# A four-layer graph network on one core: two more neighbour blocks gathered, operands moved in SBUF, rows asked for singly

## The chip, the core and the metric

The kernel runs on one NeuronCore of a Trainium2 chip. Its engines work side by side: TensorE (PE, with its weight loads PEld), VectorE (DVE), ScalarE (ACT), GpSimd (POOL) and SyncE (SP), which only starts transfers. The metric is the time of one execution on the device in microseconds, lower is better; the numbers of before are the median of three runs and one profiled execution.

## The reference

There are 6250 nodes of 256 features and 100000 edges, sorted by destination. Cut to what matters:

```python
def agg(h):
    return segment_sum(h[src], dst, num_segments=N)      # sum over a node's in-edges

h = maximum(layernorm(x), 0)
for l in range(3):
    t = relu((h + agg(h)) @ W1s[l] + b1s[l])
    t = relu(t @ W2s[l] + b2s[l])
    h = t @ W3s[l] + b3s[l]
t = relu((h + agg(h)) @ cW1 + cb1)
t = relu(t @ cW2 + cb2)                                   # 64 wide
return x + t @ cW3 + cb3
```

Since the sum over neighbours is linear, the kernel applies a layer's first weight matrix before it aggregates: W3 of one layer and W1 of the next are multiplied into one matrix, and each layer aggregates rows that are already weighted.

## The kernel before

The nodes lie in 49 blocks of 128. There are four aggregations, called layers 0 to 3 here. The features of all blocks are held in the tile `XY` (128 partitions x 49 blocks x 512 numbers): the first 256 numbers of a block are the features rounded for the fast matmul type (f32r), the other 256 are the remainder, so that two products together keep the precision.

A block of destinations is aggregated in one of two ways, which do not depend on each other:

- **Dense.** The number of edges from each source to each destination of a block is a count matrix, 49 x 128 x 128 bytes. In layer 0 it is built on the chip (`build`: one-hot rows on VectorE, L1034, multiplied at L1075, cast to bytes at L1083 and L1085) and stored to DRAM (`mats`); layers 1 to 3 fetch it again (`fetch`, L1105). Before a product the bytes are cast to f32r in a ring of tiles `a` (L1549 in layer 0, L1565 later). A panel of four blocks is one product of 49 x 4 matmuls with `XY` stationary and `a` moving (L1665); a single block ("solo", and every block in layer 0) is 49 matmuls with `a` stationary and `XY` moving (L1588). All of these are 128 x 128 by 512 columns.
- **Gathered.** For a block, 17 indirect DMAs (L1382) on the POOL queue each bring 128 rows of 1 KB, one per edge, from the DRAM copy of the features (`table`) into buffers `rows`. One-hot matrices (`one_hots`, L1402, on VectorE) and 23 small matmuls, 46 instructions in the trace (L1419), sum them in two "visits". L1439 and L1448 add the block itself.

Both ways end in the same rest: a transpose (L1479) or the product's own layout, ReLU, the second matmul (L1232), the third (L1289, in layer 3 L1244) and the store to the next table.

Which block goes which way stands in lists. `gone` (L468) are the groups that can be gathered, `panels` (L469) the dense panels, `teams` (L476) the dense blocks of layer 0 in order, `solos` (L470) the dense single blocks of layers 1 to 3, `stock` (L471) everything with a count matrix. `Gathered.blocks` (L1340) takes every block of `gone` that is not dense in that layer: 22 in layer 0, 18 in layers 1 and 2, 19 in layer 3, 77 in all and 77 x 17 = 1309 gathers. `order` (L1490) is the sequence of panels and solos in a layer.

The order of the work is written out by hand and instruction by instruction, with a planner's clock (`passed`) that adds fixed costs for what has been put on TensorE: `COLS` per column of a dense matmul, `VISIT`, `TURN` and others (L1508). From `work_of`, the planned length of a layer, `begin` derives `pace`, the planned time between two rows. `flow` (L1370) then asks for rows `LEAD` (21 us) before they are due; each gather carries a wait for the latest matmul (`after`, `paced`). In layers 1 to 3 the number asked for is rounded down to a multiple of `TRAIN`, 4. A visit is put between dense matmuls when its time on the clock has come (`meets`), or in any case in the last 8 units of a layer; if its rows have not been asked for, they are asked for there. A layer's first gather can only follow once the table of that layer is stored whole.

POOL does nothing but gathers in the layers. The row buffers are `gath` (24) in layer 0 and `gath2` (26) later. SyncE starts all other transfers.

Where the tiles lie in a partition follows from the order of the pools and the sizes in them. Before, `XY` starts at byte 16544, which is 160 modulo 256; the tiles `a` start at 193760 + k x 2048 (`rings`, layer 0; 224 modulo 256) and at 182688 + k x 2048 (`rings2`, layers 1 to 3; 160 modulo 256). The step from one block of `XY` to the next is 2048 bytes and from one stationary slice to the next 512 bytes, so these residues hold for every matmul of a kind.

Of the kernel before, what the change touches and what calls it, by code (L numbers as in the profile page):

```python
# [10 lines left out]
U8 = mybir.dt.uint8  # L11
# [6 lines left out]
P = 128  # L18
# [378 lines left out]
def sorted_edges(  # L397
# [69 lines left out]

    gone = [(0, 4), (4, 4), (8, 4), (12, 4), (16, 4), (44, 4), (48, 1)]  # L468
    panels = [(20, 4), (24, 4), (28, 4), (32, 4), (36, 4), (40, 4), (44, 4)]  # L469
    solos = [[], [17, 18, 19], [17, 18, 19], [18, 19]]  # L470
    stock = panels + [(b, 1) for b in solos[1]]  # L471
    place_of = {b + i: (p, i) for p, (b, n) in enumerate(stock) for i in range(n)}
    S0 = 2 * min(place_of)


    teams = [(17, 3), (20, 4), (24, 4), (28, 4), (32, 4), (36, 4), (40, 2), (42, 2)]  # L476
    made = [b + i for b, n in teams for i in range(n)]
    for i in range(panels[-1][1]):
        made.insert(6 * i + 5, panels[-1][0] + i)
# [7 lines left out]
    const = ctx.enter_context(tc.tile_pool(name="const", bufs=1))  # L487
    dram = ctx.enter_context(tc.tile_pool(name="dram", bufs=1, space=DRAM))
    ps_g = ctx.enter_context(tc.tile_pool(name="ps_g", bufs=1, space=PSUM))
    ps_m = ctx.enter_context(tc.tile_pool(name="ps_m", bufs=2, space=PSUM))  # L490

    XY = const.tile([P, NT, 2 * C], F32R, name="XY")
    ident = const.tile([P, P], F32, name="ident")
    clT = const.tile([P, 2, GSUB, NSUB - S0], BF16, name="clT")
# [111 lines left out]
    def ask(n):  # L606

        for _ in range(min(n, len(asks))):
            to, e, at = asks.pop(0)
            got = nc.gpsimd.indirect_dma_start(  # L610
                out=to, out_offset=None, in_=e.rearrange("(o e) -> o e", o=1),
                in_offset=bass.IndirectOffsetOnAxis(ap=at, axis=1),
            )
            after(got, "edges are asked for a few at a time")

    def look(pool):
# [200 lines left out]
        for w, (q0, q1) in ((3, (0, NQ - 1)), (4, (NQ - 1, NQ))):  # L817
            rows = gone[q0][1] * T
            nc.vector.tensor_reduce(wrong[:rows, w:w + 1], off[:rows, q0:q1, :],
                                    axis=mybir.AxisListType.XY, op=OP.max)  # L820
        ask(len(asks))
# [26 lines left out]
    def verdict():  # L848
        bad = ps_m.tile([P, W], F32, name="ps")
        nc.tensor.matmul(bad[:1, :5], one, wrong, start=True, stop=True)  # L850
        return bad

    def judge(bad):
        nc.vector.tensor_reduce(amiss, bad[:1, :5], axis=mybir.AxisListType.X, op=OP.add)
        nc.vector.tensor_scalar(good, amiss, 0.0, None, op0=OP.is_equal)


    def normed(pool, ps_t, ps_z):
# [54 lines left out]
        def times(s):  # L913
# [8 lines left out]
            if s == len(pairs) - 1:  # L922
                still = ps_m.tile([P, W], F32, name="ps")
                for _ in range(10):
                    nc.tensor.matmul(still, XY[:, 1, :P], XY[:, 0, :], start=True, stop=True)

# [6 lines left out]
        def high(s):  # L933
            i0, n = pairs[s]
            nc.scalar.copy(XY[:, i0:i0 + n, :C], zs[s][:, :n, :])

        def low(s):
            i0, n = pairs[s]
            nc.vector.tensor_tensor(XY[:, i0:i0 + n, C:], zs[s][:, :n, :],
                                    XY[:, i0:i0 + n, :C].bitcast(F32), OP.subtract)  # L940

# [21 lines left out]
    with tc.manual_schedule():  # L963
        with tc.tile_pool(name="prep", bufs=2) as prep, tc.tile_pool(
            name="ps_t", bufs=2, space=PSUM
# [146 lines left out]
        def later(n, fn):  # L1112
            due.append((now[0] + n, fn))
# [25 lines left out]
        def tick(layer):  # L1139

            now[0] += 1
            run = [f for t, f in due if t <= now[0]]
            due[:] = [(t, f) for t, f in due if t > now[0]]
            for f in run:
                f()
            visit = layer.meets()
            for task in list(jobs):
                first, last, fn = task
                if max(first, lock[0]) <= now[0] and (visit or last <= now[0]):
                    jobs.remove(task)  # L1150
                    fn()
            if queue:
                step(visit)
# [5 lines left out]
        def split(j, m, z):  # L1159

            nc.scalar.copy(XY[:, j:j + m, :C], z[:, :m, :])
            later(1, lambda: nc.vector.tensor_tensor(XY[:, j:j + m, C:], z[:, :m, :],
# [171 lines left out]
        class Gathered:  # L1334
# [35 lines left out]
            def flow(self):  # L1370

                if self.first is not None:
                    n = int((clock[0] - self.first + LEAD) / self.pace) + 1
                    self.send(n if n >= len(self.order) or not self.l else n - n % TRAIN)

            def send(self, upto):
                while self.sent < min(upto, len(self.order)):
# [109 lines left out]
        EARLY = 8  # L1487
        PRE = (GSUB + EARLY) // 2
        tails = [7] + [panels[-1][1]] * NLAYER
        order = [[]] + [[0, 17, 1, 18, 2, 3, 19, 4, 5, 6]] * 2 + [[0, 1, 18, 2, 3, 19, 4, 5, 6]]  # L1490
        order = [[p if p < len(panels) else place_of[p][0] for p in o] for o in order]
        nodes = [b + i for b, n in teams for i in range(n)]
        parts = [(j, 1) for j in range(NT)]
# [13 lines left out]
        LEAD, TAIL = 21.0, 10.0  # L1507
        COLS, FULL32, TURN, VISIT, BUILD, BURST = 0.457e-3, 1.68e-3, 0.4, 1.7, 0.2, 0.3  # L1508
        clock = [0.0]
        FAR, SPAN, TRAIN = 7, 6, 4  # L1510

        ends = [sum(1 for k, *_ in units if k <= l) for l in range(NLAYER + 1)]
        layers = [Gathered(l) for l in range(NLAYER + 1)]
# [98 lines left out]
        def product_of_team(b0, n, ps_a, beside, hurry):  # L1612
            us, h1 = [], []

            def turn(i, two):
                if not h1:
                    h1.append(work.tile([P, KC, W], F32, name="h1", bufs=2) if hurry else
                              ats.tile([P, KC, W], F32, name="h1", bufs=1))
                turned(0, two, h1[0], i)
                if i == n - 1:  # L1620
                    mlp(0, b0, n, h1[0], hurry, FAR)

            for i in range(n):
                us.append(spare[:, i * C:(i + 1) * C] if hurry else
                          ats.tile([P, C], F32, name="un", bufs=4))
                if not hurry:
                    product_by_node(0, (b0 + i,), ps_a, us[i:], beside)
                elif i == n - 1:
                    product_by_node(0, pieces[-1], ps_a, us, beside)
                if i % 2 or i == n - 1:  # L1630
                    two = us[i - i % 2:i + 1]
                    if hurry:
                        def soon(i=i, two=two):
                            if now[0] < lock[0] or sum(len(g["steps"]) == 2 for g in queue) > 1:
                                later(1, soon)
                            else:
                                turn(i, two)

                        later(3, soon)
                    else:  # L1640
                        job(FAR - 2, FAR - 2 + SPAN, lambda i=i, two=two: turn(i, two))
# [51 lines left out]
        with tc.tile_pool(name="hots", bufs=1) as hots, tc.tile_pool(  # L1693
            name="ats", bufs=1
        ) as ats, tc.tile_pool(name="rings", bufs=AHEAD + 2) as rings, tc.tile_pool(
            name="gath", bufs=24
        ) as gath, tc.tile_pool(
            name="ps_a", bufs=2, space=PSUM
        ) as ps_a, tc.tile_pool(name="ps_b", bufs=3, space=PSUM) as ps_b:
            begun = {0: clock[0]}  # L1700
            layers[0].begin()
            layers[0].send(layers[0].upto[1])
            beside = build(hots, ats, ps_b)
            while now[0] < PRE:
                for _ in range(2):
                    next(beside)
                    built[0] += 1
                tick(layers[0])
                layers[0].advance()
            later(1, lambda: later(2, lambda bad=verdict(): judge(bad)))  # L1710
            for team in teams:
                product_of_team(*team, ps_a, beside, team == teams[-1])
            assert next(beside, None) is None and built[0] == total
        chunks = ctx.enter_context(tc.tile_pool(name="chunks", bufs=1))
        late = ctx.enter_context(tc.tile_pool(name="late", bufs=1))
        rings = ctx.enter_context(tc.tile_pool(name="rings2", bufs=AHEAD + 6))
        gath = ctx.enter_context(tc.tile_pool(name="gath2", bufs=26))
        ps_a = ctx.enter_context(tc.tile_pool(name="ps_a2", bufs=4, space=PSUM))
        for l in range(1, NLAYER + 1):
            for p in order[l]:  # L1720
# [7 lines left out]
def kernel(  # L1728
# [26 lines left out]
    good = keep.tile([1, 1], I32, name="good")  # L1755
    rest = (x, src, dst, W1s, b1s, W2s, b2s, W3s, b3s, cW1, cb1, cW2, cb2, cW3, cb3, out)
    sorted_edges(tc, good, *rest)
    done = nc.values_load(good[0:1, 0:1], min_val=0, max_val=1)  # L1758
    with tc.If(done == 0):
# [27 lines left out]
```

## Time and profile before

| what | value |
|---|---|
| three runs | 2186.52 us median, 2184.53 to 2191.45 |
| profiled execution | 2191.15 us |
| its span, first to last instruction | 2189.4 us |
| mean granted TensorE clock | 0.986 |
| gathers (L1382) | 1309, mean 991 ns |
| dense matmuls (L1665 and L1588) | 4116 + 1715 |
| DMA, mean | 155 GB/s |

The span is some 2 us shorter than the execution, which holds the start and the end of the program as well. A matmul's duration in the trace (396 ns for a dense one) is longer than its distance to the next, because matmuls overlap in the array: what a matmul costs is read from how close two start. "Issue" is time in which an engine waited for nothing that the profile shows. SP and POOL rows with DMA names are the issuing, not the transfer.

### The profile page before, as it was taken

What the parts mean: (1) busy time and instruction counts of PE and PEld (TensorE: products, weight loads), DVE (VectorE), ACT (ScalarE), POOL (GpSimd) and SP (SyncE); (2) the same over time, 40 slices, a digit from 0 to 9 for tenths busy, and PEclk for the clock granted to TensorE, in tenths of its full rate; (3) what the DMA queues carried; (4) which work ended last, traced back from release to release, by engine and by line L of the source; (5) the groups of instructions that cost most, each with busy time, mean ns of one, the idle gap of its engine ahead of it and who ended that gap; (6) DMA issues with size and microseconds to landing.
All of it is one profiled execution on the core that took longest, in us unless ns stands there. A gap on an engine that the chain in (4) does not pass through costs nothing. (4 is left out here: it accounts for less than half of the span.)

```text
span 2189.4 us, 32889 instructions
## 1 busy us (share of the span) xinstructions
PE 2110.3 (96%) x12123; PEld 1530.8 (70%) x12123; DVE 951.4 (43%) x2230; ACT 892.6 (41%) x1834; POOL 1354.5 (62%) x1385
## 2 busy tenths in 40 slices
PE   4989999999999999999998999999999999999998
PEld 3756766667667777777775777777776677677675
DVE  7987767676663422222233322222223333233333
ACT  4856656565555523223333433232323333223222
POOL 2736666776763466666665266666666177777773
PEclk9989999999999999999999999999999999999999
DMA  4534444545445654445444544545455455566454
GB/s 156 169 103 147 143 143 143 155 138 153 146 147 163 189 158 146 148 136 173 149 153 141 173 152 136 166 137 167 129 164 174 134 173 190 180 195 187 155 176 130
DMA packets 182129, 340.44 MB, mean 155 GB/s; under 512 B 31246, under 2 KB 117296, under 8 KB 181958
## 3 DMA queue, kind: packets, MB, share of 16 engines
q0 software_dynamic: 64880, 174.27, 27.0%
q1 hardware_dynamic: 115150, 162.13, 22.5%
q8 instruction: 97, 1.59, 0.3%
q10 hardware_dynamic: 1928, 1.85, 0.3%
q14 instruction: 74, 0.61, 0.1%
HBM read 280.05 MB, written 58.07 MB: 154 GB/s over the span
## 5 line engine op out<-in xcount | busy, mean ns | idle before, releaser
L1382 POOL DMA_INDIRECT rows<-table,idx x1309 | 1297.7, 991 | 757.8 <-issue 272.7
L1665 PE MATMUL agg<-a,XY 128*128 128x512 f32 x4116 | 981.8, 396 | 2.0 <-ACT a L1565 2.0
L1665 PEld LDWEIGHTS agg<-a,XY 128*128 128x128 f32 x4116 | 767.5, 189 | 206.1 <-issue 37.3
L1565 ACT CAST a<-at 128x512 fp32r<-128x512 uint8 (+1 forms) x571 | 343.7, 616 | 594.7 <-PE agg L1665 537.8
L1565 DVE CAST a<-at 128x512 fp32r<-128x512 uint8 (+1 forms) x570 | 250.2, 442 | 563.6 <-PE agg L1665 462.6
L1588 PE MATMUL agg<-XY,a 128*128 128x512 f32 x1715 | 469.1, 410 | 0.6 <-ACT a L1549 0.6
L1588 PEld LDWEIGHTS agg<-XY,a 128*128 128x128 f32 x1715 | 305.0, 190 | 64.8 <-issue 10.9
L1419 PE MATMUL sums<-rows,hot 128*32 128x256 f32 x3542 | 249.1, 387 | 21.2 <-DMA rows<-table,idx 19.9
L1419 PEld LDWEIGHTS sums<-rows,hot 128*32 128x32 f32 x3542 | 107.0, 110 | 145.6 <-issue 53.2
L1549 ACT CAST a<-at 128x512 fp32r<-128x512 uint8 (+2 forms) x375 | 204.5, 575 | 6.2 <-PE agg L1588 6.2
L1083 ACT CAST at<-bp 128x392 uint8<-128x392 f32 x248 | 120.8, 488 | 202.1 <-PE bp L1075 193.8
L1085 DVE CAST at<-bp 128x392 uint8<-128x392 f32 x248 | 140.0, 565 | 139.4 <-PE bp L1075 138.4
L1448 DVE TENSOR_TENSOR u<-u,sums 128x256 f32<-128x256 f32 x77 | 32.3, 419 | 253.3 <-PE agg L1665 220.0
L1075 PE MATMUL bp<-hi,lo 128*128 128x196 bf16 x992 | 132.6, 255 | 9.9 <-DVE hi L1034 9.6
L1034 DVE TENSOR_TENSOR hi<-cols,pairs 128x784 bf16<-128x784 bf16 x248 | 139.3, 562 | 0.0
L1289 PE MATMUL ps<-w,h 128*128 128x256 f32 x588 | 133.9, 380 | 1.9 <-ACT h L1483 1.0
L1232 PE MATMUL ps<-h,w 128*128 128x512 f32 (+4 forms) x332 | 134.1, 546 | 0.7 <-DVE zz L1297 0.6
L1075 PEld LDWEIGHTS <-lo 128*128 128x128 bf16 x992 | 73.1, 99 | 84.8 <-DVE hi L1034 27.9
L1289 PEld LDWEIGHTS ps<-w,h 128*128 128x128 f32 x588 | 110.9, 190 | 18.5 <-ACT h L1483 1.5
L1483 ACT ACTIVATE h<-ps,bias 128x256 f32<-128x256 f32 (+1 forms) x118 | 47.5, 460 | 155.7 <-PE ps L1479 155.5
L1034 DVE TENSOR_TENSOR lo<-lanes,pairs 128x512 bf16<-128x512 bf16 x248 | 103.8, 419 | 1.3 <-ACT pairs L1029 1.3
L1232 PEld LDWEIGHTS ps<-h,w 128*128 128x128 f32 (+1 forms) x332 | 60.4, 189 | 54.7 <-issue 49.0
(171 smaller groups left out, 971.4 us busy)
## 6 DMA issues: line engine op xcount, KB each, us to landing
at<-mat SPq DMA_DIRECT2D x155, 448.0 KB
mat<-at SPq DMA_DIRECT2D x31, 784.0 KB
rows<-table,idx POOLq DMA_INDIRECT x1309
table<-zz SPq DMA_DIRECT2D x71, 256.0 KB
back<-table SPq DMA_DIRECT2D x99, 128.0 KB
xs<-in_x_dram SPq DMA_DIRECT2D x8, 768.0 KB
table<-zs SPq DMA_DIRECT2D x24, 256.0 KB
out_dram<-zz SPq DMA_DIRECT2D x24, 256.0 KB
```

Source lines behind the costliest of these rows:

```text
L1034: nc.vector.tensor_tensor(o.rearrange("p q (n t) -> p q n t", t=2), values.rearrange("p (n t) -> p n t", t=2)[:, None, :, :].to_broadcast( ...
L1075: mm = nc.tensor.matmul(bp[:, m * HW:(m + 1) * HW], lo[:, q + m, :], hi[:, q + m, :], start=True, stop=True)
L1083: nc.scalar.copy(o, v)
L1085: nc.vector.tensor_copy(o, v)
L1232: mm = nc.tensor.matmul(ps[:mp, :w], weights[l][0][:, c, i * P:i * P + mp], h1[:, c, :w], start=(c == 0), stop=(c == KC - 1))
L1289: mm = nc.tensor.matmul(o, h2[0][:, c, nodes], w3[:, c, :], start=(c == 0), stop=(c == KC - 1))
L1382: got = nc.gpsimd.indirect_dma_start(out=t, out_offset=None, in_=tables[self.l][:, :], in_offset=bass.IndirectOffsetOnAxis(ap=idx[:, o:o + ...
L1419: nc.tensor.matmul(self.sums[m * Q:(m + 1) * Q, :C], self.hot[:, (c - min(rounds)) // 2, m, :], self.rows[g, c + 4 * m], start=(c == ROUND ...
L1549: nc.scalar.copy(a[:, i * m * P:(i + 1) * m * P].rearrange("p (j d) -> p j d", j=m), counts[b][:, j:j + m, :])
L1565: cast(o, at[:, :, d:d + m * P])
L1588: mm = nc.tensor.matmul(agg, a[:, d:d + P], XY[:, j, :], start=(j == 0), stop=(j == NT - 1))
L1665: mm = nc.tensor.matmul(agg[c][:, :w], XY[:, j, o:o + P], a[:, :w], start=(j == 0 and half == 0), stop=(j == NT - 1 and half == 1))
```

## The change

It has four parts.

- **Which blocks.** Solos of layers 1 and 2 shrink from 17, 18, 19 to 19 alone; the first team of layer 0 from 17, 18, 19 to 18, 19. Block 17 has no count matrix any more. Gathered blocks: 23 in layer 0, 20 in layers 1 and 2, 19 in layer 3 as before; 82 in all, 1394 gathers.
- **Order.** Layers 1 and 2 have the one solo after the third panel.
- **Fillers.** A tile of 96 bytes ahead of `XY`, one of 64 bytes ahead of the ring of layer 0, one of 128 bytes ahead of the ring of layers 1 to 3. They are never written or read. With block 17 gone, `clT` is 128 bytes smaller. `XY` comes to byte 16640, the rings to 193792 and 182784, the row buffers behind them to 204032 and 201216: all 0 modulo 256.
- **Rows.** The rounding to trains of four goes, so rows are asked for one by one, and `gath2` has 25 buffers.

```diff
-    solos = [[], [17, 18, 19], [17, 18, 19], [18, 19]]
-    stock = panels + [(b, 1) for b in solos[1]]
+    solos = [[], [19], [19], [18, 19]]
+    stock = panels + [(b, 1) for b in max(solos, key=len)]
...
-    teams = [(17, 3), (20, 4), (24, 4), (28, 4), (32, 4), (36, 4), (40, 2), (42, 2)]
+    teams = [(18, 2), (20, 4), (24, 4), (28, 4), (32, 4), (36, 4), (40, 2), (42, 2)]
...
+    const.tile([P, 96], U8, name="align")
     XY = const.tile([P, NT, 2 * C], F32R, name="XY")
...
             def flow(self):
 
                 if self.first is not None:
-                    n = int((clock[0] - self.first + LEAD) / self.pace) + 1
-                    self.send(n if n >= len(self.order) or not self.l else n - n % TRAIN)
+                    self.send(int((clock[0] - self.first + LEAD) / self.pace) + 1)
...
-        order = [[]] + [[0, 17, 1, 18, 2, 3, 19, 4, 5, 6]] * 2 + [[0, 1, 18, 2, 3, 19, 4, 5, 6]]
+        order = [[]] + [[0, 1, 2, 19, 3, 4, 5, 6]] * 2 + [[0, 1, 18, 2, 3, 19, 4, 5, 6]]
...
-        FAR, SPAN, TRAIN = 7, 6, 4
+        FAR, SPAN = 7, 6
...
             begun = {0: clock[0]}
+            rings.tile([P, 64], U8, name="align", bufs=1)
...
         rings = ctx.enter_context(tc.tile_pool(name="rings2", bufs=AHEAD + 6))
-        gath = ctx.enter_context(tc.tile_pool(name="gath2", bufs=26))
+        rings.tile([P, 128], U8, name="align", bufs=1)
+        gath = ctx.enter_context(tc.tile_pool(name="gath2", bufs=25))
```

## The prediction

> **What bounds the kernel now.** I read the page first: the span, the busy times of the engines and the costliest groups.
>
> ```profile
> span 2189.4 us, 32889 instructions
> ...
> PE 2110.3 (96%) x12123; PEld 1530.8 (70%) x12123; DVE 951.4 (43%) x2230; ACT 892.6 (41%) x1834; POOL 1354.5 (62%) x1385
> ...
> L1665 PE MATMUL agg<-a,XY 128*128 128x512 f32 x4116 | 981.8, 396 | 2.0 <-ACT a L1565 2.0
> ...
> L1588 PE MATMUL agg<-XY,a 128*128 128x512 f32 x1715 | 469.1, 410 | 0.6 <-ACT a L1549 0.6
> ...
> L1419 PE MATMUL sums<-rows,hot 128*32 128x256 f32 x3542 | 249.1, 387 | 21.2 <-DMA rows<-table,idx 19.9
> ...
> L1075 PE MATMUL bp<-hi,lo 128*128 128x196 bf16 x992 | 132.6, 255 | 9.9 <-DVE hi L1034 9.6
> ```
>
> TensorE is busy 96% of the span, and two thirds of that is the dense product with the count matrices (L1665 for panels of four blocks, L1588 for single blocks). That is an average over four layers, so next come the gathers of each layer: the instructions on the tile `rows`, in four windows. Duration is min/median/max in ns, then the first and last start.
>
> ```profile
> L1382 POOL DMA_INDIRECT rows<-table,idx x374: 947/953/1583, 123.5 to 682.0; - x187
> L1382 POOL DMA_INDIRECT rows<-table,idx x306: 947/953/1291, 733.5 to 1189.8; - x153
> L1382 POOL DMA_INDIRECT rows<-table,idx x306: 947/953/1323, 1237.7 to 1697.4; - x153
> L1382 POOL DMA_INDIRECT rows<-table,idx x323: 949/953/1552, 1741.1 to 2161.1; - x162
> ```
>
> The layer periods, first gather to next layer's first gather, are 610.0, 504.2 and 503.4 us; between a layer's last gather and the next layer's first lie 51.5, 47.9 and 43.7 us (the last sums, the last products, the store of the table). Then the groups by line for POOL, in the windows of layers 0 to 3: busy time, mean ns, idle time and what ended it.
>
> ```profile
> L1382 POOL DMA_INDIRECT rows<-table,idx x374 | 375.6, 1004 | 201.0 <-PE bp L1075 73.7 <-PE agg L1588 48.5 <-issue 43.5
> L1382 POOL DMA_INDIRECT rows<-table,idx x306 | 300.5, 982 | 207.1 <-issue 71.9 <-PE agg L1665 64.4 <-DMA back<-table 50.3
> L1382 POOL DMA_INDIRECT rows<-table,idx x306 | 299.5, 979 | 208.1 <-issue 71.6 <-PE agg L1665 61.9 <-DMA w<-w 46.9
> L1382 POOL DMA_INDIRECT rows<-table,idx x323 | 322.1, 997 | 141.5 <-issue 85.6 <-DMA clT<-in_L_gnn_cb_dram 42.7 <-PE agg L1665 6.8
> ```
>
> In layers 0 to 2 POOL waits for TensorE (the pace that the program sets). In layer 3 it does not: apart from the 42.7 us before the first gather it is idle 98.8 us over 322 steps, 0.307 us each, nearly all of it "issue", and a gather comes every 420.0/322 = 1.304 us. Layer 3 has its gathers back to back; that is their floor. The chain of waits in order of time starts there too, and two rows of the list of waits show TensorE waiting for rows 57 us in all:
>
> ```profile
> 2159.82 0.95 POOL rows L1382
> 2160.77 0.30 issue
> 2161.08 4.15 DMA rows<-table,idx
> 2165.27 1.05 PE sums L1419 x10
> ```
> ```profile
> PEld sums L1419 <- DMA rows<-table,idx: 37.2, 40, 3.6
> ...
> PE sums L1419 <- DMA rows<-table,idx: 19.9, 16, 3.1
> ```
>
> So layers 0 to 2 are bound by TensorE, layer 3 by TensorE and the gather queue together.
>
> **The change, part by part.** First, five dense products go: block 17 in layer 0, blocks 17 and 18 in layers 1 and 2. The price of a dense matmul is its distance to the next, not its duration. From the timeline of PE, late in layer 0 and in layer 1 (start, length, count):
>
> ```profile
> 657.51 0.51 PE L1075 MATMUL bp<-hi,lo 128*128 128x196 bf16 x4
> 657.80 1.18 PE L1588 MATMUL agg<-XY,a 128*128 128x512 f32 x4
> 658.82 0.51 PE L1075 MATMUL bp<-hi,lo 128*128 128x196 bf16 x4
> ...
> 663.17 3.62 PE L1289 MATMUL ps<-w,h 128*128 128x256 f32 x16
> ...
> 667.65 1.50 PE L1419 MATMUL sums<-rows,hot 128*32 128x256 f32 x24
> 669.09 8.67 PE L1588 MATMUL agg<-XY,a 128*128 128x512 f32 x36
> ...
> 679.99 5.87 PE L1588 MATMUL agg<-XY,a 128*128 128x512 f32 x24
> ...
> 693.01 1.89 PE L1289 MATMUL ps<-w,h 128*128 128x256 f32 x8
> ```
> ```profile
> 984.51 7.44 PE L1588 MATMUL agg<-XY,a 128*128 128x512 f32 x32
> ...
> 1000.75 2.88 PE L1665 MATMUL agg<-a,XY 128*128 128x512 f32 x12
> ```
>
> In layer 0, 36 take 8.67 and 24 take 5.87: 2.80/12 = 233 ns each. In layer 1, 32 and 12: 4.56/20 = 228 ns. A product is 49 matmuls: 49 x 233 = 11.4 us in layer 0, 49 x 228 = 11.2 later. Block 17's counts are not built either: a group of four L1075 and four L1588 takes 658.82 - 657.51 = 1.31 us, less 4 x 0.233 leaves 0.38, and a block has 32 of the 992: eight groups, 3.0 us.
>
> What comes in: five gathered blocks, 46 sums matmuls each. The row of L1419 gives 249.1/77 = 3.2 us for each of the 77 blocks (a visit, 667.65 to 669.09, is 1.44, and there are two). Transposes and the two later matmuls see the same columns as before, only grouped otherwise: nothing. On TensorE: layer 0 -11.4 - 3.0 + 3.2 = **-11.2 us**; layers 1 and 2 -22.4 + 6.4 = **-16.0 us** each; layer 3 nothing.
>
> VectorE loses a product's add and the building of a block and gets two one-hots and two adds a block; it and ScalarE are at 391.56 and 338.43 of 560 us in their busiest layer, so they stay hidden. If not, the builds of layer 0 would hold TensorE first.
>
> ```profile
> 130.00:690.00 560.00, 551.96 (x3628) 383.06 (x3628) 391.56 (x900) 338.43 (x775) 370.58 (x369) 0.99 0.47 145
> ```
>
> Second, the fillers. The operands of the dense matmuls are XY, at residue 160 of 256 bytes throughout, and the ring tile `a`: residue 224 in layer 0, 160 in layers 1 to 3. The same L1588 with the same XY takes 233 ns in the first case, with no building beside it in the run of 36, and 228 in the second. So an address of an operand moves the price. Both go to residue 0, which no matmul of this line has here. What is left at residue 0 no row shows. The nearest: L1289, 256 columns of f32 at (3.62 - 1.89)/8 = 216 ns, which I read as 512 steps, two a column; and L1075, 196 columns of bf16 at (0.51 - 0.255)/3 = 85 ns, 222 for 512. So 216 is the floor, and the gain is 17 ns in layer 0 and 12 later at most; the other end is 0, and below 0 under the rivals. I take the full gain, because the one difference in address that the trace has already moved the price by 5 ns: layer 0 1274 x 17 = 21.7 us, layers 1 and 2 1421 x 12 = 17.1 each, layer 3 1470 x 12 = 17.6, all on TensorE.
>
> The Trainium skill, TensorE: Matmul & The Clock Gate, "Back-to-back issue gap", gives 512/2.4 + 2.5 = 215.8 ns for a lone matmul of 512 columns; the rows read above come to 216 and 222. The same page, "Step-by-step: what each phase is for", speaks against the fillers: stationary and moving operand have read ports of their own, so that loading weights takes nothing from the running matmul. By that rule where `a` lies would not matter; the 233 beside 228 of this trace disagrees. The rule's outcome is the first rival.
>
> Third, the gather queue must follow. Layer 1 asks for 340 rows instead of 306. At its own 0.982 us and layer 3's 0.307 us between two, that is 340 x 0.982 + 339 x 0.307 = 438, cut to 437 with layer 2's 0.979; with the 47.9 and 43.7 us behind it, periods of 485 and 481 us cannot be undercut. TensorE alone would need 504.2 - 16.0 - 17.1 = 471. So POOL takes over: **-19 and -22 us**. Layer 3 has the same 323 gathers at the same floor: **-1** (matmuls of the tail). Layer 0: 391 x 1.004 + 390 x 0.307 = 512, plus some 16 us in which the first rows wait for the first sums, is 528; TensorE asks for 558.5 - 11.2 - 21.7 = 526: **-29 us**. What was a TensorE bound in three layers becomes a gather bound.
>
> Fourth, trains of four become single rows. In layers 1 and 2 a row is then asked for up to three steps earlier; where POOL is saturated, as above, that is hidden, and it costs nothing since the layer-3 gathers keep 0.307 us between two whatever they wait for. One row buffer less (25 for 26): a visit uses 11 or 12, so the next visit's still fit. Nothing is queued behind a gather on POOL but gathers.
>
> **Sum**: -29 - 19 - 22 - 1 = -71 us. From the profiled execution's 2191.15 (1.75 of it outside the span) this is 2120.1; its median of runs is 4.6 lower, 2186.52, so **2115.5**.
>
> **Rivals.** (1) *The fillers do nothing*: spacing stays 233 and 228. TensorE bounds layers 0 to 2 (488 over 485 and 481): -11 - 16 - 16 = -43, **2143.5**. For it: XY and `a` share residue 160 in layers 1 to 3, and 228 may be what this kind of matmul costs. Against: 233 beside 228.
> (2) *The gathers cost more when asked for singly* (slower). Layer 0 asks singly now and its gathers lie 558.5/373 = 1.497 us apart. Were that the cost of asking and not the pace, layers 1 and 2 would take 339 x 1.497 + 47.9 = 555 and 551, layer 3 62 more: with layer 0's -29, **2318**. It decides against the change from s = 1.365 us a gather on, where -29 + (339 s + 47.9 - 504.2) + (339 s + 43.7 - 503.4) + (322 s - 420) is 0. Against it: POOL's idle time in layer 0 is put to `PE bp` and `PE agg`, and 0.95 + 0.30 is the same there.
> (3) *Operands that start alike collide*, +11 ns instead: 5586 x 11 = 61 over -43, **2204**. Against: the equal residues of layers 1 to 3 are the quicker ones.
> (4) *The gathers get quicker* (all at the median 953 ns, so 428 us for 340): -33 - 28 - 31 - 13 = -105, **2081**. Against: 997 mean in layer 3, whose other work does not change.
>
> **Numbers.** Forecast 0.54, holding 2097 to 2133 with half the filler gain or some stretch of the gathers; (1) 0.31; (2) 0.06; (3) 0.03; (4) 0.04; the rest, 0.02, no change. A measurement here tells 0.3%, about 7 us, from nothing. Faster: 0.54 + 0.31 + 0.04 = 0.89; same 0.02; slower 0.06 + 0.03 = 0.09. The range takes in the forecast and rival 1 with a few us of waiting: 2097 to 2150.
>
> **What would show it.** Dense matmuls 216 ns apart in layer 0 and later; first gathers at about 704, 1190 and 1670 us, the last at 2090; in layers 1 and 2 POOL idle 0.3 us between gathers and hardly for `PE agg`; more than 57 us of waits for rows on TensorE, in layer 3 above all. A spacing of 228 in layers 1 to 3 with POOL still waiting for TensorE would make rival 1 right; gathers over 1.365 us apart with nothing but "issue" between them, rival 2. I am wrong in the main if the POOL floor does not hold in layers 1 and 2.

## The result and the profile after

The changed kernel takes 2131.71 us (median, 2127.35 to 2135.8) against 2186.35 us (2184.53 to 2191.45) of the kernel before: **ratio 0.9746, 95% interval 0.9719 to 0.9773**. That is 55 us less, where the forecast said 71; it lies between the forecast and rival 1. The profiled executions show the same: 2191.15 to 2135.8 us, a difference of 55.35.

The page of the changed kernel, the same lines as before (line numbers from L1034 to L1290 are one higher):

```profile
span 2134.0 us, 33393 instructions
...
PE 2057.4 (96%) x12076; PEld 1487.8 (70%) x12076; DVE 937.7 (44%) x2192; ACT 864.3 (41%) x1775; POOL 1445.4 (68%) x1470
...
L1665 PE MATMUL agg<-a,XY 128*128 128x512 f32 x4116 | 982.8, 395 | 1.9 <-DVE clT L1600 1.9
...
L1588 PE MATMUL agg<-XY,a 128*128 128x512 f32 x1470 | 404.9, 409 | 1.3 <-DVE un L1600 0.7
...
L1419 PE MATMUL sums<-rows,hot 128*32 128x256 f32 x3772 | 256.0, 385 | 16.2 <-DMA rows<-table,idx 15.0
```

The panels (L1665) are the first thing to look at, because nothing of the change touches their number: 4116 before and after, 981.8 us busy before and 982.8 after. Fillers that took 12 ns from each would have shown here. The solos (L1588) fall by 245 instructions, the five products. The sums (L1419) rise by 230 instructions and only 6.9 us, because the waits within them shrink.

The gathers of each layer after the change, as durations (min/median/max, ns) and first and last start, in the four windows:

```profile
L1382 POOL DMA_INDIRECT rows<-table,idx x391: 947/954/1789, 126.6 to 674.2; - x196
L1382 POOL DMA_INDIRECT rows<-table,idx x340: 948/953/3534, 719.2 to 1163.3; - x170
L1382 POOL DMA_INDIRECT rows<-table,idx x340: 947/953/1331, 1205.7 to 1647.6; - x170
L1382 POOL DMA_INDIRECT rows<-table,idx x323: 947/953/1582, 1686.8 to 2105.0; - x162
```

| | layer 0 | layer 1 | layer 2 | layer 3 |
|---|---|---|---|---|
| first gather to the next layer's first, before (layer 3: to the end) | 610.0 | 504.2 | 503.4 | 448.3 |
| the same, after | 592.7 | 486.5 | 481.1 | 447.2 |
| difference; forecast | -17.3; -29 | -17.7; -19 | -22.3; -22 | -1.1; -1 |
| spacing of gathers, before | 1.497 | 1.496 | 1.507 | 1.304 |
| spacing of gathers, after | 1.404 | 1.310 | 1.304 | 1.299 |

The differences sum to 58.4; ahead of the first gather 3.1 us came back. That start also varies where nothing of it differs (121.8 to 126.6 us in the profiles of the kernel before, the changed one and e1 to e8), so I read nothing into it; counted from the start of the span, layer 1 begins 14.3 us earlier.

A second account goes by the matmuls: the distances from each to the next, summed by kind over the span, from all the starts in the trace. Products of L1588: 434.1 to 373.6 us, -60.5. Panels: 967.0 to 966.8. Building: 86.8 to 84.8, -2.0. Sums: 258.7 to 259.8, +1.1. All else: +6.2. Two terms stand out against the forecast: the panels gained nothing, and five more gathered blocks cost 1.1 us where 16.0 had been put down. The second has most of its reason in the list of waits, TensorE's for rows, after the change:

```profile
PEld sums L1419 <- DMA rows<-table,idx: 27.5, 27, 3.8
PE sums L1419 <- DMA rows<-table,idx: 15.0, 12, 3.3
```

These two rows must not be added. Where the weight load (PEld) waits for a row, the matmul behind it (PE) waits as well, as here in the kernel before:

```profile
1866.44 0.37 PEld L1419 LDWEIGHTS sums<-rows,hot 128*32 128x32 f32 x11 [2.95 <-DMA rows<-table,idx]
1866.44 2.46 PE L1419 MATMUL sums<-rows,hot 128*32 128x256 f32 x16 [2.47 <-DMA rows<-table,idx]
```

In the traces of the kernel before, the changed one and e1 to e8 every wait of PE for rows lies inside one of PEld, so the time lost is the first row alone: 27.5 us, against 37.2 before. From here on, waits for rows are those of PEld. So three questions went to the chip: what are blocks, fillers and single asking worth alone; why do the fillers not bring 216 ns; is the gather floor real.

### The profile page after: what moved, and what is told of

Read it like the earlier page. It is cut to its first block, busy times and chain, and to the rows that moved or that the text cites. A ratio compares the mean times of both kernels' runs of the same rounds, so it can differ in the third digit from the quotient of the medians.

```text
span 2134.0 us, 33393 instructions
## 1 busy us (share of the span) xinstructions
PE 2057.4 (96%) x12076; PEld 1487.8 (70%) x12076; DVE 937.7 (44%) x2192; ACT 864.3 (41%) x1775; POOL 1445.4 (68%) x1470
## 3 DMA queue, kind: packets, MB, share of 16 engines
q1 hardware_dynamic: 113838, 158.12, 22.3%
## 4 chain that ended last, share of the span: by engine, by line
PE 88%; DVE 5%; DMA 4%; issue 1%; ACT 1%; POOL 1%; SPq 0%; DVEq 0%; POOLq 0%; ACTq 0%
PE agg L1665 43%; PE agg L1588 16%; PE sums L1419 11%; PE ps L1233 6%; PE ps L1290 6%; PE bp L1076 4%; DMA rows<-table,idx 3%; PE ps L1479 1%; POOL rows L1382 1%; DVE junk L695 1%; PE bp L920 1%; DVE hi L1035 1%; DVE at L1086 1%; PE ps L1245 0%; DMA table<-zs 0%
## 5 line engine op out<-in xcount | busy, mean ns | idle before, releaser
L1382 POOL DMA_INDIRECT rows<-table,idx x1394 | 1387.7, 995 | 611.4 <-issue 220.6
L1665 PE MATMUL agg<-a,XY 128*128 128x512 f32 x4116 | 982.8, 395 | 1.9 <-DVE clT L1600 1.9
L1665 PEld LDWEIGHTS agg<-a,XY 128*128 128x128 f32 x4116 | 764.6, 188 | 209.5 <-issue 45.8
L1565 ACT CAST a<-at 128x512 fp32r<-128x512 uint8 (+1 forms) x542 | 326.9, 616 | 576.9 <-PE agg L1665 543.9
L1565 DVE CAST a<-at 128x512 fp32r<-128x512 uint8 x543 | 242.7, 448 | 552.8 <-PE agg L1665 469.3
L1588 PE MATMUL agg<-XY,a 128*128 128x512 f32 x1470 | 404.9, 409 | 1.3 <-DVE un L1600 0.7
L1588 PEld LDWEIGHTS agg<-XY,a 128*128 128x128 f32 x1470 | 258.9, 189 | 53.7 <-issue 8.7
L1419 PE MATMUL sums<-rows,hot 128*32 128x256 f32 x3772 | 256.0, 385 | 16.2 <-DMA rows<-table,idx 15.0
L1419 PEld LDWEIGHTS sums<-rows,hot 128*32 128x32 f32 x3772 | 112.6, 109 | 142.6 <-issue 53.6
L1549 ACT CAST a<-at 128x512 fp32r<-128x512 uint8 (+2 forms) x362 | 196.7, 574 | 6.5 <-PE agg L1588 6.5
L1448 DVE TENSOR_TENSOR u<-u,sums 128x256 f32<-128x256 f32 x82 | 34.3, 419 | 241.8 <-PE agg L1665 226.9
L1076 PE MATMUL bp<-hi,lo 128*128 128x196 bf16 x960 | 127.5, 255 | 11.0 <-DVE hi L1035 10.7
L1290 PE MATMUL ps<-w,h 128*128 128x256 f32 x588 | 133.9, 379 | 1.4 <-ACT h L1236 0.9
L1233 PE MATMUL ps<-h,w 128*128 128x512 f32 (+3 forms) x332 | 133.9, 545 | 0.6 <-DVE zz L1298 0.6
L1290 PEld LDWEIGHTS ps<-w,h 128*128 128x128 f32 x588 | 111.1, 190 | 18.7 <-ACT h L1236 1.8
L1298 DVE TENSOR_TENSOR zz<-ps,w 128x512 f32<-128x512 f32 (+1 forms) x75 | 50.1, 678 | 117.0 <-PE ps L1290 117.0
```

The lines of the kernel that those rows point to most:

```text
L1076: mm = nc.tensor.matmul(bp[:, m * HW:(m + 1) * HW], lo[:, q + m, :], hi[:, q + m, :], start=True, stop=True)
L1233: mm = nc.tensor.matmul(ps[:mp, :w], weights[l][0][:, c, i * P:i * P + mp], h1[:, c, :w], start=(c == 0), stop=(c == KC - 1))
L1290: mm = nc.tensor.matmul(o, h2[0][:, c, nodes], w3[:, c, :], start=(c == 0), stop=(c == KC - 1))
L1382: got = nc.gpsimd.indirect_dma_start(out=t, out_offset=None, in_=tables[self.l][:, :], in_offset=bass.IndirectOffsetOnAxis(ap=idx[:, o:o + ...
L1419: nc.tensor.matmul(self.sums[m * Q:(m + 1) * Q, :C], self.hot[:, (c - min(rounds)) // 2, m, :], self.rows[g, c + 4 * m], start=(c == ROUND ...
L1549: nc.scalar.copy(a[:, i * m * P:(i + 1) * m * P].rearrange("p (j d) -> p j d", j=m), counts[b][:, j:j + m, :])
```

## The experiments

Two comparisons of four kernels each, both with the kernel before beside them; a third follows at the end. Ratios are to the kernel before of the same comparison, with 95% intervals.

| kernel | us, median | ratio |
|---|---|---|
| e1, change without fillers | 2136.54 | 0.9759 (0.9740 to 0.9778) |
| e2, change with trains of four | 2136.95 | 0.9771 (0.9748 to 0.9793) |
| e3, before with single asking alone | 2173.77 | 0.9930 (0.9912 to 0.9949) |
| e4, before with the blocks alone | 2147.67 | 0.9805 (0.9785 to 0.9825) |
| kernel before, first comparison | 2190.83 | |
| e5, change with rings 64 bytes on | 2138.46 | 0.9766 (0.9747 to 0.9784) |
| e6, 21 blocks gathered in layers 1, 2 | 2163.09 | 0.9879 (0.9862 to 0.9895) |
| e7, 19 blocks gathered in layers 1, 2 | 2141.22 | 0.9781 (0.9765 to 0.9798) |
| e8, change without the pacing wait | 2123.30 | 0.9691 (0.9671 to 0.9712) |
| kernel before, second comparison | 2188.15 | |

### e1: the change without the fillers

```diff
-    const.tile([P, 96], U8, name="align")
...
+    const.tile([P, 128], U8, name="align")
...
-            rings.tile([P, 64], U8, name="align", bufs=1)
...
-        rings.tile([P, 128], U8, name="align", bufs=1)
```

The one filler that is put in stands behind `clT` and makes up for its 128 bytes, so `XY` and both rings have the residues of before: 160, and 224 and 160.

> The changed kernel (2131.7 us) with its operands back where they lay before: XY at residue 160, the rings at 224 (layer 0) and 160. Theory A, that where the operands lie is worth a few us in layer 0 alone: 2131 to 2137, long runs of dense matmuls in layer 0 at 233 ns, 227 in layers 1 to 3. The step of the prediction (17 ns in layer 0, 12 later, cut by the gather floor): about 28 us slower, 2160.

It takes 2136.54 us, ratio 0.9759 against 0.9746 with the fillers. The instructions of L1588 late in layer 0 (the last 86) and in layer 1 (the product of block 19), without the fillers (e1: count, then min/median/max in ns, then first and last start):

```profile
L1588 PE MATMUL agg<-XY,a x86: 390/395/799, 661.0 to 692.1; 128*128 128x512 f32 x86
...
L1588 PE MATMUL agg<-XY,a x49: 387/389/497, 886.0 to 902.0; 128*128 128x512 f32 x49
```

And with them, in the changed kernel:

```profile
L1588 PE MATMUL agg<-XY,a x86: 387/390/792, 662.7 to 693.6; 128*128 128x512 f32 x86
...
L1588 PE MATMUL agg<-XY,a x49: 387/389/499, 885.8 to 901.8; 128*128 128x512 f32 x49
```

In layer 0 the fillers lower the median duration from 395 to 390 ns, and from the first start to the last the 86 take 30.9 us for 31.1; in layer 1 they move nothing, 16.0 us for the 49 in both. In runs of 16 and more dense matmuls the distance settles at 233.3 ns in layer 0 and 226.7 later without the fillers, and 226.8 everywhere with them. So the fillers do what rival 1 says in layers 1 to 3, nothing, and in layer 0 they take 6.5 ns from a matmul, but only in long runs. There are few: between builds the products come in threes and fours, whose distances are set by other things, and all of layer 0's L1588 distances sum to 328.1 us for 329.8.

### e2: the change with trains of four

```diff
-                    self.send(int((clock[0] - self.first + LEAD) / self.pace) + 1)
+                    n = int((clock[0] - self.first + LEAD) / self.pace) + 1
+                    self.send(n if n >= len(self.order) or not self.l else n - n % TRAIN)
```

> The changed kernel asking for rows in trains of four again in layers 1 to 3. Theory A, that the single rows shortened TensorE's waits for rows (57 us before, 42 after) and so gave what the blocks don't explain: 2139 to 2146, with 50 us or more of waits for rows. Rival, that the extra came from elsewhere: 2130 to 2134.

2136.95 us, ratio 0.9771. TensorE waits for rows 30.1 us, 2.6 more than in the changed kernel. The intervals of 0.9771 and 0.9746 overlap, so e2 alone settles nothing; e3 does.

### e3: single asking alone

The reverse edit in the kernel before: the rounding to trains goes, the rest stays (26 buffers, 18 blocks, no fillers).

> The kernel before with nothing changed but the asking, one row at a time instead of four. Theory A: TensorE's waits for rows fall, 2174 to 2181. Rival, single rows help only where the gather queue is full: 2184 to 2189. The prediction said nothing at all, 2186.

2173.77 us, **ratio 0.9930 (0.9912 to 0.9949)**: 0.7% or 15 us from the step that the prediction put at nothing. The list of waits of e3 (its lines are one lower):

```profile
PEld sums L1418 <- DMA rows<-table,idx: 22.1, 23, 3.2
...
PE sums L1418 <- DMA rows<-table,idx: 13.0, 11, 2.7
```

22.1 us, where the kernel before has 37.2: 15 us of waiting go, by layers 1, 2 and 3: 14.1 to 8.3, 7.2 to 1.1, 15.9 to 12.7. The distances behind the matmuls of the sums say the same: 258.7 to 242.6 us, 16.1 of the 16.8 us by which the two profiled spans differ. In the kernel before, 17.8 of the 37.2 us come later than 20 us before a layer's last gather, where the last 8 units force the visits and a visit cannot run ahead of its rows; the longest wait, 3.6 us, ends there too, at 1186.3 us. With single asking 10.8 us are left there. So about half of the gain lies at the ends of the layers, the rest within them. That a row asked for one to three steps of 1.3 us earlier lands earlier is the plain explanation; no run shows it apart from the result.

### e4: the blocks alone

```diff
-    solos = [[], [17, 18, 19], [17, 18, 19], [18, 19]]
+    solos = [[], [19], [19], [18, 19]]
...
-    teams = [(17, 3), (20, 4), (24, 4), (28, 4), (32, 4), (36, 4), (40, 2), (42, 2)]
+    teams = [(18, 2), (20, 4), (24, 4), (28, 4), (32, 4), (36, 4), (40, 2), (42, 2)]
...
+    const.tile([P, 128], U8, name="align")
...
-        order = [[]] + [[0, 17, 1, 18, 2, 3, 19, 4, 5, 6]] * 2 + [[0, 1, 18, 2, 3, 19, 4, 5, 6]]
+        order = [[]] + [[0, 1, 2, 19, 3, 4, 5, 6]] * 2 + [[0, 1, 18, 2, 3, 19, 4, 5, 6]]
```

The residues, the trains and the 26 buffers stay as before.

> The kernel before with the blocks, the order and nothing else: trains of four, 26 buffers, the operands at the residues of before. By TensorE's sum (-11, -16, -16) 2143. Theory A (single rows needed for the rest): 2141 to 2148. Rival, that the blocks alone give it all: 2130 to 2136.

2147.67 us, ratio 0.9805: 0.0195 x 2188 = **42.7 us** from the blocks, where the sum for TensorE said 43. The periods are 598.4, 489.4 and 484.0 us; the forecast for TensorE alone was 488 and 487 in layers 1 and 2. Waits for rows stay at 35.9 us.

With e1, e2, e4 and the changed kernel the other two edits stand in a square:

| | trains of four | singly |
|---|---|---|
| residues as before | 0.9805 (e4) | 0.9759 (e1) |
| fillers | 0.9771 (e2) | 0.9746 (changed kernel) |

Single asking takes 0.0046 without and 0.0025 with the fillers, 10 and 5 us; the fillers take 0.0034 and 0.0013, 7 and 3 us. Each ratio is good to some 0.002, so only the direction and the rough size hold: single asking 5 to 15 us, fillers between nothing and 7. The changed kernel's ratio comes from a comparison of its own, and e4 has 26 row buffers where the other three have 25, which no run separates.

### e5: the rings 64 bytes further

```diff
-            rings.tile([P, 64], U8, name="align", bufs=1)
+            rings.tile([P, 128], U8, name="align", bufs=1)
...
-        rings.tile([P, 128], U8, name="align", bufs=1)
+        rings.tile([P, 192], U8, name="align", bufs=1)
```

`XY` stays at residue 0 and the tiles `a` come to 64. This asks whether the value of a residue counts or the distance between the two operands.

> The changed kernel with both rings 64 bytes further on, so that the tiles a stand at residue 64 and XY at 0: 64 apart in all layers, as before the change in layer 0 alone (224 and 160). Theory, that the distance between the two residues sets the price and not residue 0: long runs of dense matmuls at 233 ns in layers 1 to 3 too, 4312 x 5 = 22 us more on TensorE, part of it hidden behind the gathers of layer 3: 2142 to 2155. Rival, that the 233 ns of layer 0 had to do with something else in that layer: 227 in layers 1 to 3, 2130 to 2137.

The same two groups of L1588 in e5:

```profile
L1588 PE MATMUL agg<-XY,a x86: 390/397/799, 663.2 to 694.4; 128*128 128x512 f32 x86
...
L1588 PE MATMUL agg<-XY,a x49: 390/394/497, 888.6 to 904.8; 128*128 128x512 f32 x49
```

Now layer 1 has the slower form too: 394 ns for 389, and 16.2 us for the 49. In long runs L1588 stands at 233.3 ns in every layer, with `XY` at 0 and `a` at 64, as it did in layer 0 before with 160 and 224: 64 bytes apart both times. With equal residues, at 160 or at 0, it is 226.8. So it is the distance between the operands and not the residue 0, for the two distances tried, 0 and 64. The panels, where `XY` is the stationary operand, lose only 2.1 ns (228.9), and so the time is 2138.46 us, below the low end of what was expected: a miss in size. Over the span the panels' distances grow by 5.6 us and those of L1588 by 3.5, while those of the sums shrink by 6.2, with 22.1 us of waits for rows in place of 27.5.

The Trainium skill, TensorE: Matmul & The Clock Gate, "Step-by-step: what each phase is for", has independent read ports for the moving and the stationary operand, so that loading weights takes nothing from a running matmul. 226.8 beside 233.3 ns for one kind of matmul, with only the address of the weights moved, is 6.5 ns that this does not lead one to expect; that the weight load takes them is not shown. By "Back-to-back issue gap" on the same page of the Trainium skill a lone matmul of 512 columns would take 215.8 ns, an estimate by its formula; no run of dense matmuls in these traces settled there.

### e6 and e7: one block more, one block fewer

```diff
-    solos = [[], [19], [19], [18, 19]]
+    solos = [[], [], [], [18, 19]]
...
-        order = [[]] + [[0, 1, 2, 19, 3, 4, 5, 6]] * 2 + [[0, 1, 18, 2, 3, 19, 4, 5, 6]]
+        order = [[]] + [[0, 1, 2, 3, 4, 5, 6]] * 2 + [[0, 1, 18, 2, 3, 19, 4, 5, 6]]
```

That is e6; e7 has `[18, 19]` in layers 1 and 2 and layer 3's order in all three.

> The changed kernel with block 19 gathered too in layers 1 and 2: 21 blocks, 357 gathers, no single dense block. Theory, that layers 1 and 2 stand at the point where TensorE and the gather queue meet: gathers 1.305 us apart make 465 us a layer, with the 42 behind it 508 for 486 and 481, so 40 to 50 us slower, 2172 to 2182. Rival, that TensorE alone is the bound: another 8 us off each layer, 2112 to 2120.

> The changed kernel with blocks 18 and 19 dense in layers 1 and 2: 19 gathered, 323 gathers. Theory: TensorE has 8 us more a layer and some 4 to 6 us less waiting for rows: 2135 to 2143. Rival, that layers 1 and 2 are held by the gather queue already at 20 blocks: faster than the changed kernel, 2115 to 2128.

e6 takes 2163.09 us, 31 over the changed kernel's median (2172 to 2182 had been expected), though TensorE has a product less in two layers. The gathers of its layer 1 as a group by line, and the waits for rows:

```profile
L1382 POOL DMA_INDIRECT rows<-table,idx x357 | 353.8, 991 | 154.3 <-PE agg L1665 82.3 <-issue 57.3 <-DMA rows<-table,idx 8.8
```
```profile
PEld sums L1419 <- DMA rows<-table,idx: 71.5, 64, 3.8
...
PE sums L1419 <- DMA rows<-table,idx: 41.8, 35, 3.2
```

357 gathers 1.296 us apart take 461.4 us, and the period is 502.2; TensorE waits 71.5 us for rows, for 27.5 in the changed kernel. With 21 blocks the queue is the bound. "PE agg" stands ahead of "issue" in that row and misleads: a gather released by a matmul starts as late after the one before, 0.30 us, as one that waited for nothing. In e7, with 323 gathers, they come every 1.396 us, the waits for rows sink to 21.0 us and it takes 2141.22 us, some 9 over the changed kernel: there TensorE is the bound. The intervals of e7 and the changed kernel overlap by a little, but the periods agree with the medians: 490.2 and 486.2 us in layers 1 and 2, for 486.5 and 481.1. The crossing lies near 20, and the number in the change looks the right one of the three.

### e8: no pacing

```diff
-                    after(got, "rows are asked for evenly over a layer")
```

> The changed kernel with gathers that no longer wait for the latest matmul; they still wait for a free buffer and for the table. Measures the floor of 1.30 us a gather. Theory, that 0.95 us of work and 0.30 us between two are POOL's own: gathers as far apart in layer 3 as before, 1.298 on average, time 2125 to 2137. Rival, that the 0.30 us is the price of the wait: 1.0 us apart, no waits for rows on TensorE (42 us now), 2090 to 2115.

2123.30 us, ratio 0.9691 (0.9671 to 0.9712), the fastest here and just below what was expected; the interval lies just below that of the changed kernel. The gathers of layers 1 to 3 stay 1.297, 1.282 and 1.301 us apart, with nothing left to wait for but buffers. Over the whole program (duration as min/median/max in ns, then what ended POOL's idle time, in us and times):

```profile
L1382 POOL DMA_INDIRECT rows<-table,idx x1394: 947/953/3533, 125.8 to 2098.5; - x200
its engine sat idle before it (us, times) until:
  issue: 224.8, 734
```

734 times POOL waited for nothing that the profile shows, 0.306 us each. So the **floor is the queue's own**: the step is never under 1.25 us, 0.95 of work and 0.30 between. Waits for rows fall to 19.8 us, and layers 1 and 2 take 481.0 and 477.2 us.

### e9 to e12: steps of the ring, and the same kernels once more

```diff
-                a = rings.tile([P, W], F32R, name="a")
+                a = rings.tile([P, W + 8], F32R, name="a")[:, :W]
```

e9 makes a ring tile 2080 bytes, so that the nine tiles `a` of layers 1 to 3 take the residues 0, 32, ... 224 and 0 again in turn, beside `XY` at 0; e10 is the changed kernel, e11 is e1 and e12 is e8, each as it was.

> The changed kernel with ring tiles of 2080 bytes instead of 2048 (the 32 more are never used), so that the tiles a of one ring lie at residues 0, 32, 64 and so on up to 224 against XY at 0: every distance in one run, read tile by tile. Theory, that only the distance between the two operands counts and that 227 ns is what such a matmul takes: 227 at 0, 233 at 64, nothing below 226. Rival, that 227 still has an address in it: some residue near 216. For L1665, where XY is the stationary operand: 227 at 0 and 229 at 64, by the run with the rings 64 on.

> The changed kernel once more, on the same chip as the next two and with more rounds, as their measure. 2127 to 2136, ratio 0.9725 to 0.9765.

> The changed kernel with its operands where they lay before, on the same chip as the changed kernel. Theory: the fillers shorten dense matmuls in layer 0 by 1.5 ns in the mean (short runs between the builds) and by 6 in long runs, 2 to 4 us in all, 0.1 to 0.2% slower than the changed kernel. Rival: nothing, within 0.05%. The prediction's step: 28 us, 1.3%.

> The changed kernel without the gathers' wait for the latest matmul, on the same chip as the changed kernel. Theory, that the wait makes rows late at the ends of layers 1 and 2 and there alone: 7 to 10 us faster than the changed kernel. Rival, that the chips differed: within 3 us.

In this comparison, on the chip of the second one, every kernel was slower, the one before too (2280.99 us, 2276.21 to 2288.11, for 2188.15 then), so its times are not set beside those above. Within it the order was another: e10 2359.78, ratio 1.0340 (1.0324 to 1.0357); e11 2359.95, 1.0349 (1.0332 to 1.0366); e12 2599.17, 1.1389 (1.1363 to 1.1414); e9, a single run, 2364.88. **The changed kernel was slower than the one before here, and the version without pacing much slower.** e10 and e11 cannot be told apart, which fits fillers that are worth little.

What differs from the same kernel's earlier profile, in the list of waits of e10 (sum in us, count, longest; `remote` stands where the profile can't tell what released the engine):

```profile
PEld sums L1419 <- issue: 127.5, 253, 2.0
...
ACT a L1565 <- remote: 81.0, 30, 9.8
DVE a L1565 <- remote: 79.7, 28, 8.1
DVE a L1565 <- issue: 76.4, 27, 11.0
...
PEld sums L1419 <- DMA rows<-table,idx: 15.2, 13, 3.4
```

Earlier the first was 53.6 us, the two with `remote` did not occur, and `DVE a L1565 <- issue` was 10.1. ScalarE and VectorE stand idle up to 11 us where the profile has nothing that they wait for. Three rows from the timeline of e10:

```profile
901.88 0.60 PE L1479 MATMUL ps<-ident,u 128*128 128x128 f32 x4
...
906.52 0.43 DVE L1565 CAST a<-at 128x512 fp32r<-128x512 uint8 x1 [7.26 <-PE agg L1665]
...
909.34 0.84 ACT L1483 ACTIVATE h<-ps,bias 128x256 f32<-128x256 f32 x2 [8.19 <-PE ps L1290]
```

The transposes end at 902.5, and ScalarE takes their result at 909.34, where 0.04 to 0.4 us is usual in the earlier profile. Several times ScalarE, VectorE and POOL start again together: at 1071.9 to 1072.1 us after 7.8, 11.0 and 2.0 us, at 1105.7 to 1105.9 after 5.4, 8.1 and 2.1. The dense matmuls keep their 226.8 ns in long runs, and a gather its 0.95 us; but with casts and ReLUs late TensorE runs dry, and gathers that wait for matmuls come 1.47 us apart for 1.30. It is not the waits for rows: those shrank to 15.2 us. In e12 the same gaps are longer (up to 18.5 us before a cast), and the mean granted clock of TensorE is 0.928, for 0.966 in e10 and 0.988 in the changed kernel's earlier profile. Why the two engines start late, and why the kernel before suffers less, is not settled: there is no trace of the kernel before from this comparison.

For e9 the distances still serve, taken tile by tile, each with some 400 distances in the panels and 14 to 24 in L1588 (twice as many at residue 0). The panels' mean is least at residue 0, 231.6 ns, and most at 64, 233.1; L1588's in layers 1 to 3 lies between 231.3 and 233.7. Nothing comes near 216 at any residue. The expected split, 227 at 0 and 229 at 64 in the panels, shows in its direction only, 1.5 ns; probably, with a new residue every four matmuls, no run settles.

## Where the prediction was right, and where it was not

**What bounds the kernel, right.** TensorE in layers 0 to 2, the queue and TensorE in layer 3; e6 and e7 show both sides of the crossing. The 57 us of waits for rows are the sum of two rows that overlap; TensorE lost 37.2.

**First step, the blocks, right.** Forecast 43 us, e4 42.7. Its terms were less exact than their sum. In e4's profile the products give -58.6 us for -56.2 put down, the building -1.9 for -3.0, the sums +10.7 for +16, and the rest +7.0, which had been put at nothing. That these come to 42 again is in part luck.

**Second step, the fillers: the one that failed.** "I take the full gain" to 216 ns was the term that was mis-sized: 17 ns in layer 0 and 12 later were put down, and 6.5 ns came, in long runs of layer 0 alone, and nothing in layers 1 to 3. The observation behind it, that an address moves the price, was right; the inference was not. Two values, 233.3 and 226.8, were read as two points on the way to a floor. They were two cases, residues 64 apart and equal residues, and the better one was already there in three layers. The floor itself came from other kinds of matmul (L1289, L1075) and holds for none of the dense ones. The prediction named the sign of it, under rival 1: `XY` and `a` share residue 160 in layers 1 to 3. Net of the gather bound the step carried 28 us of the 71; the square gives 3 to 7.

**Third step, the gather floor, right in size, in part by luck.** Spacings of 1.310 and 1.304 us against the 0.307 between two plus 0.98 put down; periods of 486.5 and 481.1 against 485 and 481; layer 3 -1.1 against -1. But the gathers of layers 1 and 2 took 444 and 442 us for 437, and what lies behind them 42.4 and 39.2 for 47.9 and 43.7: two errors that cancel. Nor are 485 and 481 a bound that cannot be undercut: e8 has 481.0 and 477.2. That the queue has a floor of about 1.3 us a gather is shown by e6 and e8; that it alone sets layers 1 and 2 of the changed kernel is not. The prediction has TensorE done well ahead (471 us); with 227 ns a matmul TensorE needs 488 and 487 by the prediction's own sum, less what single asking saves, and is as full as the queue. In layer 0, where the floor does not rule, the lost filler gain shows whole: -17.3 (-14.3 from the start of the span) for -29.

**Fourth step, single asking, wrong.** That asking earlier "costs nothing" was right; that it "is hidden" was not. It gave 15 us alone (e3) and 5 to 10 with the blocks. The prediction saw that POOL is saturated and concluded that an earlier request hides in the queue. It had the waits for rows quoted and did not ask where they lie: half of them at the layer ends, where the visits are forced and each row's landing counts. Accordingly "more than 57 us of waits" came out as 42.5 by the same count, 27.5 without what is counted twice.

**The sum.** -43 for the blocks, some -13 for the other two together, is the 55 measured. The forecast came to 71 with 21 to 25 too much on the fillers and 5 to 10 missing on single asking; that the time came this near to the forecast owes something to these two errors having opposite signs. All of this holds for the result and for e1 to e8; beside e10 the kernel before was the faster one, for a reason that stays open.

**Rivals.** (1) was right about the spacing in layers 1 to 3, and its 2143.5 is 12 us too high for the same missing single asking. (2) fell: gathers asked for singly come every 1.30 us, and e3 is faster. (3) fell: equal residues are the quicker ones. (4) fell: mean durations are 993, 983 and 994 ns in layers 1 to 3, for 982, 979 and 997.

## What to carry to other kernels

Before counting on an alignment, look whether another stage of the same kernel already has it: if operands at equal residues show a spacing, that spacing is the result, and what other kinds of matmul reach is no floor for this one. When work moves from one engine to a queue, work out the queue's floor as steps of busy time plus the gap, add what lies between layers, and stop at the crossing: one block past it cost some 30 us here, one short of it some 9. And where a wait is in the profile, find its place before calling an edit to its supplier hidden, and count it once where two engines stand still for the same thing.

## What was not expected of the hardware

A dense f32r matmul of 512 columns takes 226.8 ns when its two operands start at equal addresses modulo 256, and 233.3 (`XY` moving) or 228.9 (`XY` stationary) when they lie 64 bytes apart. At equal addresses the first nine or so after a break come about 231 ns apart before the distance settles at 227.

A gather is stretched by VectorE work that reads two operands from SBUF. Averaged over the changed kernel's layers 1 to 3, a gather that overlaps a one-hot (L1402) lasts 183 ns more than its 953, one that overlaps L1439 184 more; beside L1448, which reads one operand from PSUM, it is 4. Gathers beside a cast of L1565 and none of the two-operand instructions last 20 ns longer. Two rows from the timeline of the changed kernel:

```profile
1310.11 0.55 DVE L1402 TENSOR_TENSOR hot<-colf,rel 128x384 f32<-128x384 f32 x1
1310.23 1.26 POOL L1382 DMA_INDIRECT rows<-table,idx  x1 [0.30 <-issue]
```

The gather takes 1.26 us for 0.95. The Trainium skill, SBUF — State Buffer, "SBUF: two separate sides", has one port pair that VectorE and GpSimd share under an exclusive lock, taken also by a VectorE instruction with two SBUF inputs against a GpSimd one that reads SBUF; a gather reads `idx` there, and these rows and the 183 and 184 against 4 ns agree. Of the 37 us by which the 1003 gathers of layers 1 to 3 exceed 953 ns each, 29 fall on the 187 beside a VectorE instruction with two operands in SBUF and 8 on those beside casts alone; this makes the mean of a gather 0.98 to 0.99 us there, and the step about 1.30 rather than 1.25.

And a program can run for a whole comparison with ScalarE and VectorE starting late for no reason that the profile shows, and the faster of two kernels can then be the slower.
